# A gated layer's order of pieces on the matmul engine, written anew

## The chip, the cores and the metric

The kernel runs on one NeuronCore of a Trainium2 chip. The core has a matmul engine (PE, with its weight loads shown apart as PEld), a vector engine (DVE), an activation engine (ACT), a general engine (POOL), and queues that issue DMAs (SP, and POOL for gathers and scatters). The engines run side by side; each executes its own instructions in the order in which they were written, and semaphores make one wait for another. Matmul results land in PSUM, which DVE and ACT read; everything else lives in SBUF. The metric is the time of one launch in microseconds (us), the median over launches; a profiled launch is told apart.

## The reference, cut to what matters

The program is a stack of four layers over an activation `x` of 2048 tokens by 256. Each layer normalizes `x` and adds an attention branch and a feed-forward branch. The third layer (`L2`) is the one that is touched. Its attention branch is a gated attention with 64 slots per head, 16 heads:

```python
z = cumlogsumexp(s); g = exp(concat(z[:1], z[:-1]) - z); p = exp(s - z)   # s = clip(x @ Ws, -32, 32)
hk = hk * g_t + k_t * p_t;  ok_t = q_t @ hk          # slot scores, one step per token
pv = softmax(ok)
hv = hv * g_t + p_t * v_t;  ov_t = pv_t @ hv
o  = rmsnorm(ov) * g_norm_weight * silu(x @ Wg)      # then o @ Wo is added to x
```

Its feed-forward branch is itself a small block: a latent attention (16 heads of 16, causal, with rotary parts), a residual, a root-mean-square norm, a shared expert and two of seven routed experts:

```python
h   = x + attention(rmsnorm(x, ln1))
out = h + shared(rmsnorm(h, ln2)) + routed(rmsnorm(h, ln2))
```

## The kernel before, in words

The gated attention is cut into 32 units: 8 pairs of heads times 4 blocks of 512 tokens. The recurrences are written as chunks of 128 tokens, so a unit is a chain of matmuls with small DVE and ACT steps between. Three generators emit it, and each `yield` ends a piece of PE work:

- `gated_supply` (lines 1361 to 1395, pieces "s"): the projections `Wk`, `Ws`, `Wq` of a coming unit (line 1371), the clamp (1381), exponential (1382), running sum `rz` (1383) and its four reciprocals on DVE (1384), and the transposes `kt` and `eT` (`turned`, 1402).
- `gated_unit` (pieces "m"): key scores `sc` (line 1440), values `Wv` (1455), chunk sums `ke` and `ev` (1422), slot scores inside the chunk and between chunks (1475 and 1481, giving `pok`), the product `ok` on DVE (1485), its transposes `okt` (1489), the softmax on DVE and ACT (1493 to 1499), gates `Wg` (1455, silu on ACT 1503), the transposes `pvt` (1507) and `q2` (1511), second scores (1440), and the output `pov` in two steps (1518 and 1525). What follows `pov` is squares on ACT (1535), products and sums on DVE (1536, 1539), and a scale by POOL (1541 to 1548) that finishes the unit's `o`.
- `gated_drain` (pieces "d"): the transposes `ot` of that `o` (line 1561, copied by ACT at 1562) and two halves of `o @ Wo` (1568) added to `x` on DVE (1573).

A list, `GATED` (and `LAST` for the last unit), says in which order the pieces of three chains follow on PE: the unit itself ("m"), the supply of the next unit, the drain of the unit before. Each entry holds the chain, the array size that its matmuls use (A for 128 by 128, B for 64 rows, C for 64 columns), and an assumed length in us. All PE instructions keep the order in which they are emitted; the other engines' orders are chosen by the framework's scheduler from its own estimates.

Other work runs beside the units: `latent_chain` (line 1678) during the first 24, then the routed experts `routed2`, then parts of the next layer. The class `Beside` (line 107) decides before each gated piece whether pieces of that other work go in. It keeps a credit (filled in proportion to the gated time emitted) and a weight per piece. Wide pieces are of kind A; the latent key scores come as narrow pieces E (32 rows, `qk` at 1778 for the maxima, `kq` at 1810 for the exponentials), F (32 columns, `pv` at 1826) and K (the keys, 1737 to 1754). A narrow piece goes in where the array size turns anyway, and at least 1.8 us, by the planner's own lengths (`PIECE`), after the last narrow one. A wide piece has no such distance: among them are the transposes `mxt` (1795), which need the maxima, and the transposes of the latent `pvs` (1836).

At the end of a block of tokens the latent chain emits, as wide pieces: transposes `att` (1853), the projection `op` (1860) added to `xn` on DVE (1865), then the norm (squares on ACT 1690, a sum on POOL 1876 and a power on POOL 490 and 491, the scaling on DVE 1693), the transposes `tr` of the normed rows (552), the router's `lg` (1883, 1889) and the shared expert (1906, 1189).

PSUM is held in pools of four banks: one pool, tag `ps`, for all gated pieces, one, tag `w`, for the latent chain. A piece can start when the bank that was handed out four requests earlier has been read. In SBUF most gated tiles have a single buffer.

Of the kernel before, what the change touches and what calls it, by code (L numbers as in the profile page):

```python
# [7 lines left out]
F32 = mybir.dt.float32  # L8
# [36 lines left out]
class Ring:  # L45
# [40 lines left out]
    ("m", "B", 1.1), ("m", "A", 1.8), ("m", "A", 1.8), ("s", "A", 1.8), ("m", "C", 0.5), ("m", "C", 0.8),  # L86
    ("m", "C", 0.9), ("m", "A", 0.7), ("s", "A", 1.8), ("d", "A", 0.9), ("m", "A", 0.5), ("m", "A", 1.8),
    ("m", "A", 1.8), ("m", "A", 0.5), ("s", "A", 1.8), ("m", "B", 1.1), ("m", "B", 0.8), ("s", "A", 0.5),
    ("m", "A", 1.8), ("d", "A", 1.8), ("s", "A", 0.5), ("d", "A", 1.8),
)  # L90
LAST = (
    ("m", "B", 1.1), ("m", "A", 1.8), ("m", "A", 1.8), ("m", "C", 0.5), ("m", "C", 0.8), ("m", "C", 0.9),
    ("m", "A", 0.7), ("d", "A", 0.9), ("m", "A", 0.5), ("m", "A", 1.8), ("d", "A", 1.8), ("d", "A", 1.8),
    ("m", "A", 1.8), ("m", "A", 0.5), ("m", "B", 1.1), ("m", "B", 0.8), ("m", "A", 1.8),
)
PIECE = {"A": 1.0, "E": 1.3, "F": 2.0, "K": 4.1}
# [10 lines left out]
class Beside:  # L107
# [3 lines left out]
    def __init__(self, pieces, apart=1.8, early=4.0):  # L111
        self.pieces, self.apart, self.early = pieces, apart, early
        self.ahead = next(pieces, None)
        self.now, self.narrow, self.credit, self.before = 0.0, -9.0, 0.0, "A"

    def go(self):
        self.ahead = next(self.pieces, None)

    def between(self, after):

        while self.ahead:
            kind, weight = self.ahead
            turn = self.before != after
            if self.credit < weight - (self.early if turn and kind != "A" else 0.0):
                break
            late = self.credit >= 4.5 + weight and "A" in (self.before, after)
            if kind == "A":
                if "A" not in (self.before, after):
                    break
            elif self.now - self.narrow < self.apart or not (turn or late):  # L130
                break
            self.credit -= weight
            self.order = self.before
            self.go()
            self.now += PIECE[kind]
            if kind != "A":
                self.narrow = self.now
            self.before = {"A": "A", "K": "B" if self.order == "A" else "A"}.get(kind, kind)
# [6 lines left out]
    def finish(self):  # L145
        while self.ahead:
            self.order = self.before
            kind = self.ahead[0]
            self.go()
            self.before = {"A": "A", "K": "B" if self.order == "A" else "A"}.get(kind, kind)  # L150


class Net:
# [1042 lines left out]
    def layer2(self):  # L1196
# [9 lines left out]
        with ExitStack() as ctx:  # L1206
# [8 lines left out]
            def supplied(u):  # L1215
# [5 lines left out]
                units[u] = {"b": b, "w": weights[pair]}  # L1221
                return self.gated_supply(units[u])
# [9 lines left out]
            def run(u, beside, count):  # L1232


                supply = supplied(u + 1) if u + 1 < UNITS else iter(())
                drain = self.gated_drain(units[u - 1]) if u else iter(())
                chains = {"m": self.gated_unit(units[u]), "s": supply, "d": drain}
                order = [p for p in (GATED if u + 1 < UNITS else LAST) if u or p[0] != "d"]
                rate = count / sum(us for _, _, us in order)
                for what, kind, us in order:  # L1240
                    beside.between(kind)
# [5 lines left out]
            for it in (norms[0], supplied(0)):  # L1247
                for _ in it:
                    pass
            with ExitStack() as lctx:  # L1250
# [111 lines left out]
    def gated_supply(self, t):  # L1362
# [15 lines left out]
        nc.scalar.copy(t["kT"], project("Wk"))  # L1378
        yield
# [4 lines left out]
        inverse = lambda c: nc.vector.reciprocal(rz[:, c * P : (c + 1) * P], rz[:, c * P : (c + 1) * P])  # L1384
# [862 lines left out]
```

## Time and profile before

| | us |
|---|---|
| median of 3 launches (2227.93 to 2236.01) | 2228.69 |
| the profiled launch | 2251.34 |
| its span, first to last instruction | 2249.6 |
| PE busy in the span | 1903.3 |
| DVE busy | 1221.3 |
| ACT busy | 894.5 |
| POOL busy | 639.1 |
| the 1000 us from 540 to 1540: PE busy | 941.21 |
| the same: DVE, ACT, POOL busy | 579.45, 443.71, 166.85 |

The page's 40 slices show the gated layer as the stretch from about 490 to 1870 us: PE is busy eight or nine tenths in every slice there, DVE five or six, ACT four, DMA nearly none until 1540. A busy figure of PE counts a matmul from its issue to its modelled end, at whatever clock was granted, so it contains time in which the array ran slowly. A line of the view by waits reads: who waited, for whom, total us, number of times, longest. In the timeline each row is a run of equal instructions with its start, its length, and in brackets the idle time before it and what ended that.

### The profile page before, as it was taken

To read this page: it belongs to the slowest core of one execution; us is meant where nothing else is said; L and a number is where in the kernel's file an instruction comes from. 1 tells how busy PE (TensorE), PEld (TensorE's weight loads), DVE (VectorE), ACT (ScalarE), POOL (GpSimd) and SP (SyncE) were. 2 spreads that over 40 slices of the span, in tenths; PEclk is the share of its full clock that TensorE was granted. 3 is DMA by queue.
4 is the path that set the end of the run, shared out by engine and by line. 5 is a ranking of instruction groups with operands and counts; after the bars stand their busy time and mean duration, and the time that the engine had idled before them with its cause. 6 is when DMAs were issued, how large, how long until landed. Compare 5 with 4: busy or idle time off the path is not lost.

```text
span 2249.6 us, 35179 instructions
## 1 busy us (share of the span) xinstructions
PE 1903.3 (85%) x12844; PEld 1422.2 (63%) x12844; DVE 1221.3 (54%) x3593; ACT 894.5 (40%) x1828; POOL 639.1 (28%) x762
## 2 busy tenths in 40 slices
PE   6843388848999999999999999988889978799995
PEld 2511377726666676667666666666777866578994
DVE  6752367667655665555655566548546574422222
ACT  1340155523434534434444444453345433234321
POOL 5347544451121211112112112111434441022231
PEclk9965699979999999999999999999999989789998
DMA  9944389850000000000000000001433310167696
GB/s 286 306 138 162 130 272 309 282 183 1 8 10 6 8 10 6 6 13 5 6 13 6 3 15 24 6 10 51 135 120 118 109 50 1 41 227 263 216 330 230
DMA packets 145083, 231.46 MB, mean 103 GB/s; under 512 B 15156, under 2 KB 107670, under 8 KB 144758
## 3 DMA queue, kind: packets, MB, share of 16 engines
q1 hardware_dynamic: 130822, 188.74, 26.3%
q0 software_dynamic: 14064, 40.23, 5.2%
q8 instruction: 107, 1.75, 0.3%
q14 instruction: 90, 0.74, 0.1%
HBM read 178.07 MB, written 66.19 MB: 109 GB/s over the span
## 4 chain that ended last, share of the span: by engine, by line
PE 61%; DVE 10%; DMA 7%; POOL 6%; issue 6%; SPq 5%; ACT 4%; POOLq 0%; DVEq 0%; another core or an unknown queue 0%; ACTq 0%
PE pt L1455 7%; PE pj L1371 6%; SPq L469 5%; PE g L1998 5%; PE o L1568 4%; PE kq L1810 3%; PE sc L1440 3%; POOL l_rows L338 3%; PE pov L1525 3%; PE qk L1778 2%; PE gu L1165 2%; PE o L2011 2%; DMA l_rows<-xn,at 2%; DMA r<-l_rows,in_slot 2%; PE pv L1826 2%
## 5 line engine op out<-in xcount | busy, mean ns | idle before, releaser
L446 POOL DMA_INDIRECT l_outs<-y,to x156 | 153.5, 984 | 276.2 <-ACT y L445 157.4
L1785 DVE CUSTOM_DVE_ANT_0 junk<-qk,hide 128x512 f32<-128x512 f32 (+3 forms) x256 | 124.5, 486 | 73.0 <-PE qk L1778 53.3
L1455 PE MATMUL pt<-Wg,xnT 128*128 128x256 f32 x512 | 131.4, 410 | 9.0 <-DVE eF L1381 9.0
L1818 POOL TENSOR_SCALAR_AFFINE_SELECT pr<-pr 128x512 f32<-128x512 f32 x64 | 40.2, 640 | 343.6 <-ACT pr L1815 328.4
L1998 PEld LDWEIGHTS g<-rT,we 128*128 128x128 f32 x1120 | 131.9, 194 | 5.3 <-ACT rT L439 3.2
L1998 PE MATMUL g<-rT,we 128*128 128x128 f32 x1120 | 132.8, 277 | 1.7 <-ACT rT L439 1.7
L396 POOL DMA_INDIRECT r<-l_rows,in_slot x73 | 71.2, 976 | 211.1 <-PE rt L437 99.7
L1455 PE MATMUL pt<-Wv,xnT 128*128 128x256 f32 x512 | 122.8, 390 | 0.0
L408 DVE TENSOR_TENSOR mine<-r,number 128x2 f32<-128x2 f32 (+2 forms) x90 | 16.4, 183 | 195.8 <-DMA r<-l_rows,in_slot 190.6
L1568 PE MATMUL o<-Wo,oT 128*128 128x256 f32 x512 | 122.5, 383 | 0.0
L439 ACT COPY rT<-rt 128x256 f32<-128x256 f32 x156 | 57.9, 372 | 157.9 <-remote 75.8
L1455 PEld LDWEIGHTS pt<-Wg,xnT 128*128 128x128 f32 x512 | 102.3, 207 | 25.5 <-DVE eF L1381 10.0
L1165 PE MATMUL gu<-rT,we 128*128 128x128 f32 x664 | 94.8, 288 | 25.4 <-ACT rT L439 13.4
L1446 DVE TENSOR_TENSOR s<-sc,keep 128x512 f32<-128x512 f32 x128 | 82.7, 683 | 60.2 <-PE sc L1440 59.5
L1384 DVE RECIPROCAL rz<-rz 128x128 f32<-128x128 f32 x128 | 114.6, 926 | 0.3
L1165 PEld LDWEIGHTS gu<-rT,we 128*128 128x128 f32 x664 | 88.8, 200 | 39.5 <-ACT rT L439 21.2
L1455 PEld LDWEIGHTS pt<-Wv,xnT 128*128 128x128 f32 x512 | 95.7, 193 | 16.6 <-PE kq L1810 1.5
L445 ACT ACTIVATE y<-o,share 128x256 f32<-128x256 f32 x156 | 73.6, 472 | 80.6 <-PE o L2011 43.4
L1568 PEld LDWEIGHTS o<-Wo,oT 128*128 128x128 f32 x512 | 97.1, 198 | 10.1 <-issue 1.7
L1815 ACT ACTIVATE pr<-kq 128x512 f32<-128x512 f32 (+1 forms) x192 | 85.7, 531 | 44.4 <-PE kq L1810 44.1
L1458 ACT COPY v<-pt 128x512 f32<-128x512 f32 x64 | 37.6, 588 | 150.5 <-PE pt L1455 150.5
L1810 PE MATMUL kq<-q,kT 32*128 32x128 f32 (+3 forms) x512 | 86.1, 475 | 5.2 <-DVE mx L1785 5.0
(502 smaller groups left out, 4478.3 us busy)
## 6 DMA issues: line engine op xcount, KB each, us to landing
we<-l_packed SPq DMA_DIRECT2D x121, 384.0 KB
we<-l_w SPq DMA_DIRECT2D x70, 512.0 KB
we<-l_wo SPq DMA_DIRECT2D x35, 512.0 KB
l_rows<-none SPq DMA_DIRECT2D x1, 13917.5 KB
r<-l_rows SPq DMA_DIRECT2D x16, 732.5 KB
xn<-l_outs SPq DMA_DIRECT2D x32, 256.0 KB
l_rows<-xn SPq DMA_DIRECT2D x8, 544.0 KB
l_packed<-l_w_gate SPq DMA_DIRECT2D x1, 4096.0 KB
```

Source lines behind the costliest of these rows:

```text
L446: self.no_order(moe["name"] + " back", nc.gpsimd.indirect_dma_start(out=moe["outs"][:, :], out_offset=bass.IndirectOffsetOnAxis(ap=to, axi ...
L469: self.nc.sync.dma_start(out, in_)
L1165: nc.tensor.matmul(ps[:, q, :], we[:, q, k * P : (k + 1) * P], rT[:, k, :], start=(k == 0), stop=(k == KD - 1))
L1371: nc.tensor.matmul(ps, w[n][:, k, :], self.xnT[:, k, t["b"] * T : (t["b"] + 1) * T], start=(k == 0), stop=(k == KD - 1))
L1384: inverse = lambda c: nc.vector.reciprocal(rz[:, c * P : (c + 1) * P], rz[:, c * P : (c + 1) * P])
L1446: nc.vector.tensor_tensor(s, ps[hh], keep4, ALU.mult)
L1455: nc.tensor.matmul(ps[:, i, :], self.xnT[:, k, s : s + P], w[n][:, k, :], start=(k == 0), stop=(k == KD - 1))
L1568: nc.tensor.matmul(ps[:, p, :], of_parity(oT[:, h, c * D : (c + 1) * D], p), wo[:, h, :], start=(h == 0), stop=(h == 1),)
L1785: nc.vector.tensor_tensor_reduce(out=junk[:, :m], in0=tiles[j][:, off : off + m], in1=self.hide[:, T - m :], op0=ALU.add, op1=ALU.max, sca ...
L1810: nc.tensor.matmul(tiles[j][:, BLOCK[i] - off : BLOCK[i] - off + T - i * P], kT[r, i * P : (i + 1) * P], qT[r, i * P :], start=True, stop= ...
L1815: nc.scalar.activation(pr[:, j, off : off + m], tiles[j][:, :m], AF.Exp, scale=0.25)
L1998: nc.tensor.matmul(pt[:, m, :], we[:, q, k * T + m * P : k * T + (m + 1) * P], rT[:, k, :], start=(k == 0), stop=(k == KD - 1),)
```

## The change

The order of pieces in `GATED` and `LAST` is written anew, and so are the order within two of the chains and the rule by which other work goes in.

1. In the unit ("m"), the first half of `Wv` becomes the first piece, ahead of the key scores. It is emitted at the end of the unit before (entry "n"; for the first unit, ahead of the loop). The two halves of `Wg`, two pieces with a yield between, become one piece of 3.6 us.
2. In the supply, the order `Wk`, `Ws`, `Wq`, `kt`, `eT` becomes `Ws`, `Wq`, `eT`, `Wk`, `kt`; the four reciprocals follow one piece each, from the second on.
3. In the list, `ot` moves up to stand behind the second half of `Wv`, the first half of `o @ Wo` goes between the inter-chunk scores and `okt`, the second half between `Wg` and `pvt`; `Ws` moves ahead of the inter-chunk scores; `Wq`, `eT` stand between `pvt` and the second scores, `Wk` between the two steps of `pov`.
4. Each entry gets a fourth field. Where it is 1, a wide piece of other work may go in ahead of the entry on a credit of its weight less 2; elsewhere a wide piece now needs its weight plus 1 (before: its weight everywhere). Narrow pieces may go in as early as before, at a credit of their weight less 4.
5. Distances are kept by kind (`APART`): 1.8 for E, 2.5 for F, 1.5 for K, and for two wide kinds that are now told apart, 3.0 for `mxt` ("X") and 1.5 for the transposes of `pvs` ("Y"). The assumed lengths of E and F change a little.

The matmuls are the same in number and shape, 18764 PE instructions in the program before and after.

```diff
 GATED = (
-    ("m", "B", 1.1), ("m", "A", 1.8), ("m", "A", 1.8), ("s", "A", 1.8), ("m", "C", 0.5), ("m", "C", 0.8),
-    ("m", "C", 0.9), ("m", "A", 0.7), ("s", "A", 1.8), ("d", "A", 0.9), ("m", "A", 0.5), ("m", "A", 1.8),
-    ("m", "A", 1.8), ("m", "A", 0.5), ("s", "A", 1.8), ("m", "B", 1.1), ("m", "B", 0.8), ("s", "A", 0.5),
-    ("m", "A", 1.8), ("d", "A", 1.8), ("s", "A", 0.5), ("d", "A", 1.8),
+    ("m", "B", 1.1, 0), ("m", "A", 1.8, 0), ("d", "A", 0.9, 0), ("m", "C", 0.4, 0), ("m", "C", 0.7, 0), ("m", "C", 1.0, 0),
+    ("s", "A", 1.8, 0), ("m", "A", 0.7, 1), ("d", "A", 1.8, 0), ("m", "A", 0.5, 1), ("m", "A", 3.6, 0), ("d", "A", 1.8, 0),
+    ("m", "A", 0.5, 1), ("s", "A", 1.8, 0), ("s", "A", 0.5, 0), ("m", "B", 1.1, 1), ("m", "B", 0.8, 0),
+    ("s", "A", 1.8, 0), ("m", "A", 1.8, 1), ("n", "A", 1.8, 0), ("s", "A", 0.5, 0),
 )
...
-PIECE = {"A": 1.0, "E": 1.3, "F": 2.0, "K": 4.1}
+PIECE = {"A": 1.0, "X": 0.5, "Y": 0.5, "E": 1.2, "F": 2.2, "K": 4.1}
+APART = {"A": 0.0, "X": 3.0, "Y": 1.5, "E": 1.8, "F": 2.5, "K": 1.5}
...
-    def between(self, after):
+    def between(self, after, wish):
 
         while self.ahead:
             kind, weight = self.ahead
-            turn = self.before != after
-            if self.credit < weight - (self.early if turn and kind != "A" else 0.0):
+            turn, wide = self.before != after, "A" in (self.before, after)
+            if self.now - self.narrow < APART[kind]:
                 break
-            late = self.credit >= 4.5 + weight and "A" in (self.before, after)
-            if kind == "A":
-                if "A" not in (self.before, after):
+            if kind in "AXY":
+                if not wide or self.credit < weight + (-2.0 if wish else 1.0):
                     break
-            elif self.now - self.narrow < self.apart or not (turn or late):
+            elif not turn and not (wide and self.credit >= 4.5 + weight) or self.credit < weight - 4.0:
                 break
             self.credit -= weight
...
-        nc.scalar.copy(t["kT"], project("Wk"))
-        yield
         eF, rz = t["eF"], t["rz"]
         nc.vector.tensor_scalar(eF, project("Ws"), 32.0, -32.0, ALU.min, ALU.max)
         nc.scalar.activation(eF, eF, AF.Exp)
         nc.vector.tensor_tensor_scan(rz, self.one_col.to_broadcast([P, T]), eF, 0.0, ALU.mult, ALU.add)
         inverse = lambda c: nc.vector.reciprocal(rz[:, c * P : (c + 1) * P], rz[:, c * P : (c + 1) * P])
+        yield
+        nc.scalar.mul(t["qT"], project("Wq"), 0.125)
         inverse(0)
         yield
-        nc.scalar.mul(t["qT"], project("Wq"), 0.125)
+        t["eT"] = self.turned(eF, "eT")
         inverse(1)
         yield
+        nc.scalar.copy(t["kT"], project("Wk"))
+        inverse(2)
+        yield
         t["kt"] = self.turned(t["kT"], "kt")
-        inverse(2)
-        yield
-        t["eT"] = self.turned(eF, "eT")
         inverse(3)
...
+        v = wk.tile([P, 4, D], F32, tag="v", name="v")
+        by_tokens("Wv", v, 0, nc.scalar.copy)
+        yield
         s = scores(kT, qT)
         yield
-        v = wk.tile([P, 4, D], F32, tag="v", name="v")
-        for c in (0, 2):
-            by_tokens("Wv", v, c, nc.scalar.copy)
-            yield
+        by_tokens("Wv", v, 2, nc.scalar.copy)
+        yield
...
         for c in (0, 2):
             by_tokens("Wg", g, c, lambda out, ps: nc.scalar.activation(out, ps, AF.Silu))
-            yield
+        yield
...
-                steps.append((self.latent_maxima(*maxima[2:]), list("EEEA")))
+                steps.append((self.latent_maxima(*maxima[2:]), list("EEEX")))
...
-                steps.append((self.latent_values(*values), list("EEEFA")))
+                steps.append((self.latent_values(*values), list("EEEFY")))
```

## The prediction

> **What bounds the kernel now.** First the page: busy time and the slices.
>
> ```profile
> PE 1903.3 (85%) x12844; PEld 1422.2 (63%) x12844; DVE 1221.3 (54%) x3593; ACT 894.5 (40%) x1828; POOL 639.1 (28%) x762
> PE   6843388848999999999999999988889978799995
> PEclk9965699979999999999999999999999989789998
> ```
>
> The gated layer is slices 9 to 33. PE is nearly full there, no other engine is above six tenths: PE's order is the path, and a reordering can only win or lose idle time, slow clock, and turns of the array size. The waits of PE between 540 and 1540 us, where the latent chain runs beside the units, name the idle part (who waited, for whom: us, times, longest):
>
> ```profile
> PE pvt L1507 <- ACT pv L1496: 12.5, 8, 2.2
> PE mxt L1795 <- DVE rz L1384: 12.2, 4, 3.0
> PE pt L1455 <- DVE eF L1381: 9.0, 4, 2.3
> PE mxt L1795 <- ACT pr L1815: 8.0, 9, 2.3
> PE kq L1810 <- DVE mx L1785: 5.0, 12, 0.6
> PE pvt L1836 <- ACT pvs L1832: 3.0, 2, 2.3
> ...
> PE mxt L1795 <- DVE mt L1792: 1.8, 1, 1.8
> ```
>
> All rows of that answer sum to 58. The slow clock is the second part. Stretches before, in and after one wait (length, busy us and count of each engine, granted clock, DMA):
>
> ```profile
> 1037.00:1039.75 2.75, 0.49 (x6) 0.26 (x4) 1.55 (x4) 0.90 (x4) 1.08 (x2) 1.00 0.00 0
> 1039.80:1043.20 3.40, 3.40 (x8) 2.78 (x9) 3.40 (x6) 2.80 (x5) 1.71 (x2) 0.50 0.00 0
> 1043.20:1046.60 3.40, 2.50 (x14) 1.89 (x14) 3.40 (x5) 3.10 (x4) 0.08 (x1) 1.00 0.00 0
> ```
>
> PE stood for 2.26 us, and the next 3.4 us ran at half clock: 1.7 us more. Laying stretches of 3.41 us over the layer, each of the 20 that held 2 us or more of idle time was followed by a half-clock one; of the 29 with 0.9 to 2 us, six were. From 540 to 1540 the mean clock is 0.97, so 30 us are lost that way.
>
> A third part shows in no wait. A group of value scores `kq` follows a group of maxima `qk` and takes over its four PSUM banks one by one as DVE reads them; the gaps stay under what counts as idle. A large group (2048 columns) should take 0.9 us and takes 2.4 to 4.2 when it stands 2 us of PE work behind its `qk`; summed over the layer's groups, against the duration of those that stand 5 us or more behind, the excess is 45 us.
>
> **The change part by part.** Distances below are PE work between two instructions in the built orders, priced by the trace (0.43 us per 512 columns on the full array and pass, a half or a quarter of it for B, C and E, F).
>
> *Turns.* 362 in the layer before, 384 after. Start to start, a turn adds 0.094 us: +2.
>
> *Waits that go.* `mxt` stood 0.1 us behind the last `kq`; now 3.8 to 5.6 lie between. Its 22.0 us (12.2 + 8.0 + 1.8) go. `Wg` no longer waits for a bank that the clamp holds: 9.0. `pvs` gets 1.7 us or more instead of once 0.1: 3.0. Between `okt` and `pvt` lay 3.5 us or more, now 5.2 (`Wg` and half of `o @ Wo`); the chain there (silu, table load, exponential) needed 4.9, so of 12.5 us I leave 4, in the units where DVE still has maxima ahead: 8.5 go. Sum −42.5. Thirteen half-clock stretches followed these: −22.
>
> *What is late next, 1: the feature turn after the latent output.* This decides my forecast. The rows, from the end of `op` on (timelines of PE, DVE and POOL):
>
> ```profile
> 768.18 3.30 PE L1860 MATMUL op<-both,oT 128*128 128x256 f32 x14 [0.24 <-ACT oT L1854]
> ...
> 785.12 1.04 PE L552 MATMUL tr<-ident,xn 128*128 128x128 f32 x8
> ```
> ```profile
> 771.51 0.69 DVE L1865 TENSOR_TENSOR xn<-op,xn 128x512 f32<-128x512 f32 x1 [1.03 <-PE op L1860]
> ...
> 775.89 0.88 DVE L1693 SCALAR_TENSOR_TENSOR xn<-xn,rms,ln 128x256 f32<-128x256 f32 x2 [3.02 <-POOL rms L491]
> ```
> ```profile
> 772.29 2.19 POOL L1876 TENSOR_TENSOR x<-x,xn 128x1024 f32<-128x1024 f32 x1 [12.18 <-DVE xn L1865]
> 774.56 0.19 POOL L490 TENSOR_SCALAR rms<-ms 128x4 f32<-128x4 f32 x1
> 774.84 1.02 POOL L491 TENSOR_TENSOR rms<-rms,neghalf 128x4 f32<-128x4 f32 x1
> ```
>
> The first two normed rows are ready at 776.77, 5.3 us after `op` ends (771.48); before, `tr` came 13.6 us after it. With the new credit rule wide pieces go in several at a time ahead of a flagged entry, and in the built order `tr` stands behind `op` with only half of `o @ Wo` (1.75) between, in three of four blocks, and with nothing in the fourth. Wait 5.3 − 1.75 = 3.5, and 0.3 for the second pair of rows; `lg` now follows `tr` at once and waits 0.5 for the copies; `op` itself waits some 1.6 longer, since on ACT the copy of `att` now stands behind both silus and their table loads (1.28 each). 5.9 × 3, and 8 in the fourth, where reciprocals (0.93 each) also precede the add on DVE: +26. Each block gets about two half-clock stretches, seven in all: +12.
>
> *Late next, 2: `ot`.* The chain from `pov` to a finished `o`:
>
> ```profile
> 1098.92 1.29 DVE L1536 TENSOR_TENSOR o<-pov,g 128x512 f32<-128x512 f32 x2 [2.84 <-ACT sq L1535]
> 1100.12 1.27 DVE L1539 TENSOR_REDUCE ms<-sq 128x4 f32<-128x512 f32 x2
> 1101.47 0.20 POOL L1541 TENSOR_TENSOR rs<-ms,sm 128x8 f32<-128x8 f32 x1 [3.76 <-DVE ms L1539]
> 1101.75 1.64 POOL L1545 TENSOR_TENSOR rs<-rs,neghalf 128x8 f32<-128x8 f32 x1
> 1103.47 2.04 POOL L1548 TENSOR_TENSOR o<-o,rs 128x512 f32<-128x512 f32 x2
> ```
>
> `pov` ended at 1098.4, `o` is done 7.1 later, so the first transpose must start 6.9 behind. Before, 17 to 25 us lay there; now 5.0 to 10.3. The shortfalls of the first 23 units (0.1 to 1.9) sum to 10: +10, too short to slow the clock.
>
> *Late next, 3: exponentials of the keys.* In five units a `kq` falls behind `Wg`, and the built order of ACT puts its four exponentials behind silu, load, softmax exponential, load, silu, load. Walked through with 1.28 per load and 0.6 per activation they end some 3 us after `pv` wants them: +15, and three half-clock stretches, +5. Where a `kq` stands just ahead of `ot`, the copies of `ot` come late for `pok`'s bank, 0.9 in six units: +5.
>
> *Nothing.* `kq` behind `qk`: of the 30 large groups, 15 stand under 2.4 us behind before and 14 after, which gives 45 us both ways. `eT`, `kt`, `Wk` moved: 3.5 us or more to each reader against copies of 0.6; if DVE or ACT were 3 us behind, `kt` would wait. The weight loads on SP follow in a new order (`Ws` before `Wk`), units ahead of use; DMA is at 0.03 there. On POOL only the unit's three scale steps move, behind nothing new.
>
> *Routed experts, 1540 to 1800.* `o` waits for `h` 21 us (17.4 + 1.9 + 1.8). Nine times the new order leaves 0.2 us between a block's `gu` and its `o` (before at least 1.3): silu 0.28, product 0.23 and two hand-overs want about 0.95, and five of these stand behind `Ws`, where a 1.28 load and the 1.22 scan come first: 7 + 11. `ot` adds 6, half-clock 3 more. Some 18 of the old 21 go: +9, between 0 and +18. *The end, to 1870*: a 6.5 us wait of the slot scores for `ke` goes, as ACT now copies both halves ahead of the next layer's operands; those then hold up the exponential: −4, between −10 and +4.
>
> *Sum:* −42.5 − 22 + 2 + 26 + 12 + 10 + 15 + 5 + 5 + 9 − 4 = +15.5, on the profiled launch's 2251.3 (span 2249.6): 2266.8. The median of the launches shown is 22.6 lower: **2244 us**.
>
> [...] The change has 12 more loads. [...]
>
> **The rivals.** *Paid from the hidden stall (faster).* The waits at `ot`, `pvt` and `op` fall between a `qk` and its `kq` and give DVE time to free the banks. Place: the 30 large `kq` groups; price: a group at 2 us loses 2.6, one at 3.2 loses 0.6. If all reach 3.2, 33 us of the 45 come back: 2244 − 33 = 2211. It decides once they gain half a us each on average (15 us). For it: the stalls are real and many units have such a pair. Against: the big new waits, at `tr`, have no `qk` open around them.
>
> *Moved one for one (no change).* DVE's reciprocals (0.93, four a unit) bound both orders; what `mxt` and `Wg` lose, `pvt` and `okt` get, so that the waits and clock that go (64.5) and the latent terms that come (26 + 12 + 10 + 15 + 5 + 5 + 2 = 75) cancel; only the routed part and the end are left, 2251.3 + 9 − 4 − 22.6 = 2234. For it: DVE precedes each of the waits that go. Against: PE has 2 to 5 us more distance at each.
>
> *The routed part breaks down (much slower).* Several rounds at a time empty the four-deep gather: each of some 38 blocks waits 1 us more: 2244 + 38 = 2282.
>
> **How the numbers follow.** A measurement here cannot tell less than about 0.5%, 11 us. Forecast 0.46, paid from stalls 0.32, one for one 0.17, breakdown 0.05. The forecast's own range is 2230 to 2265 (the latent terms ±20%, routed and end by their bounds). To leave no more than 2 in 10 out: 2202 to 2272. Faster 0.32; same 0.17; slower 0.51.
>
> **What would show it.** Right: `mxt` and `Wg <- eF` gone from the waits; `tr <- DVE xn` four times at 3 to 7 us with half clock behind it; `ot <- POOL o` in a dozen units, under 2 us; `pv` waiting for exponentials or their POOL mask. Wrong: `tr` without a wait, or the busy time of `kq` (86.1 before) fallen by 20 or more.

## The result, and the profile after

The changed kernel takes 2246.36 us (median of 12 launches, 2238.88 to 2251.93) against 2231.31 us for the kernel before (12 launches beside it): the ratio is 1.0066, with a 95% interval of 1.0050 to 1.0083, so 15 us more. The forecast was 2244.

Its profiled launch took 2246.59 us (span 2244.9), which is *less* than the 2251.34 us of the profiled launch before. That comparison misleads. In the trace of before, the first projection of the gated layer starts at 483.4 us, in the trace of after at 459.1: the layers ahead, which the change does not touch, happened to take 24 us longer. From the first projection of the layer to the end of the launch, the one took 1766.2 us and the other 1785.8, 19.6 more; the medians say 15, and single launches spread by some 13 us. The stages in the table below are therefore counted from that first projection. First the page of the changed kernel, busy time and slices:

```profile
PE 1914.4 (85%) x12844; PEld 1426.5 (64%) x12844; DVE 1220.4 (54%) x3585; ACT 913.8 (41%) x1848; POOL 637.6 (28%) x762
PE   6843499669999899998999899987889888799995
PEclk9965699879999899999999899998999989789997
```

The matmuls are the same (x12844 in both pages), yet PE is busy 11 us longer. As busy time runs from issue to a modelled end, this says that matmuls ran slowly (clock) or stood inside a group, not that there is more work. ACT has 19 us more, of which 15 are twelve more table loads (142 against 130) of 1.28.

The waits of PE from 540 to 1540 us, beside the latent chain (who waited, for whom: us, times, longest). As the layer starts 24 us earlier in this trace, the last rows of such a view reach into the routed part:

```profile
PE tr L549 <- DVE xn L1696: 15.4, 4, 5.5
PE kq L1813 <- DVE mx L1788: 9.7, 17, 1.5
PE op L1863 <- ACT oT L1857: 8.1, 3, 2.7
PE ot L1564 <- POOL o L1551: 3.5, 7, 0.9
...
PE mxt L1798 <- ACT pr L1818: 2.2, 3, 1.1
```

The first four rows of before (`pvt`, `mxt`, `Wg`, `mxt`: 41.7 us) are gone but for 2.2. At the top stands a wait that was not there, `tr`, four times, once for each block of tokens, as forecast.

The next table divides the launch by stage, from the traces. "Idle" is the sum of PE's gaps above 0.15 us; "clock" is half the time that the records show at half clock; "rest" is what is left. Units 0 to 22 are the stretch from the first `pov` of unit 0 to that of unit 23.

| us | before | after |
|---|---|---|
| first projection to first `pov` | 44.3 | 48.4 |
| units 0 to 22 (latent chain beside) | 994.8 | 1004.3 |
| of these: idle / clock / rest | 59.1 / 30.7 / 905.0 | 47.1 / 35.8 / 921.3 |
| units 23 to 28 (mostly routed experts) | 266.0 | 277.3 |
| from the first `pov` of unit 29 to the end of the launch | 461.1 | 455.8 |

So beside the latent chain 12 us of idle time were won, and 5 us of clock and 16 us of "rest" lost. More than half of that rest is no loss, because the borders of the table cut the two orders at different places. In the new order 16 more matmuls of `o @ Wo` and 16 more of the shared expert stand ahead of the first `pov` of unit 23; before, they stand behind it. At their mean lengths in the stage they are an estimated 9 us. With such differences taken off at each border, the stage beside the latent chain is about 1 us longer than before, units 23 to 28 about 16 us longer, the end 3 us shorter and the start 5 us longer.

Of the 7 us of rest that remain, 2 are for the 22 turns more (384 against 362, at 0.094 us each in the trace of before); the others are PE standing inside groups, in gaps that count as busy. The rows of a few groups show where, over the gated layer (busy us, mean ns | idle before), first of before, then of after:

```profile
L1810 PE MATMUL kq<-q,kT 32*128 32x128 f32 (+3 forms) x512 | 86.1, 475 | 5.2 <-DVE mx L1785 5.0 <-ACT pr L1815 0.2
L1826 PE MATMUL pv<-pr,both 128*32 128x128 f32 (+3 forms) x512 | 37.8, 436 | 0.0
L1561 PE MATMUL ot<-ident,o 128*128 128x128 f32 x248 | 32.5, 274 | 0.0
L1889 PE MATMUL lg<-rw,a2T 128*128 128x7 f32 x64 | 8.2, 263 | 0.0
```

```profile
L1813 PE MATMUL kq<-q,kT 32*128 32x256 f32 (+3 forms) x512 | 88.9, 478 | 9.9 <-DVE mx L1788 9.7
L1829 PE MATMUL pv<-pr,both 128*32 128x128 f32 (+3 forms) x512 | 37.8, 436 | 0.0
L1564 PE MATMUL ot<-ident,o 128*128 128x128 f32 x248 | 36.4, 282 | 6.6 <-POOL o L1551 5.9 <-DVE s L1446 0.7
L1892 PE MATMUL lg<-rw,a2T 128*128 128x7 f32 x64 | 12.8, 337 | 0.0
```

`kq` is busy 2.8 us longer and waits 9.7 us for the maxima instead of 5.0. `ot` took 3.9 us more with the same work; in units 0 to 22, with half clock taken off, it is 2.6. `lg` took 4.6 us more, but that is half clock, which the table has under "clock". `pv` took exactly as long and never waited.

One block's output in the changed kernel, from the timelines of PE, ACT, DVE and POOL (start, length, row, and the idle time before with its releaser):

```profile
750.63 5.47 PE L1863 MATMUL op<-both,oT 128*128 128x256 f32 x16 [2.66 <-ACT oT L1857]
755.94 1.89 PE L1571 MATMUL o<-Wo,oT 128*128 128x256 f32 x8
761.14 2.06 PE L549 MATMUL tr<-ident,xn 128*128 128x128 f32 x8 [3.31 <-DVE xn L1696]
763.13 0.62 PE L1886 MATMUL lg<-rb,ones 1*128 1x28 f32 x2
763.68 3.58 PE L1892 MATMUL lg<-rw,a2T 128*128 128x7 f32 x16
```

```profile
748.21 1.28 ACT L1506 ACT_TABLE_LOAD   x1
749.51 0.60 ACT L1506 ACTIVATE g<-pt 128x512 f32<-128x512 f32 x1
750.00 1.07 ACT L1857 COPY oT<-att 128x512 f32<-128x512 f32 x2
```

```profile
756.14 0.69 DVE L1868 TENSOR_TENSOR xn<-op,xn 128x512 f32<-128x512 f32 x1 [1.41 <-PE op L1863]
...
760.51 1.67 DVE L1696 SCALAR_TENSOR_TENSOR xn<-xn,rms,ln 128x256 f32<-128x256 f32 x4 [1.95 <-POOL rms L488]
```

```profile
756.91 2.18 POOL L1879 TENSOR_TENSOR x<-x,xn 128x1024 f32<-128x1024 f32 x1 [20.06 <-DVE xn L1868]
759.17 0.19 POOL L487 TENSOR_SCALAR rms<-ms 128x4 f32<-128x4 f32 x1
759.45 1.02 POOL L488 TENSOR_TENSOR rms<-rms,neghalf 128x4 f32<-128x4 f32 x1
```

`op` waits 2.66 us, because the copies of the transposed `att` (done at 747.97) stand on ACT behind a table load and a silu of the gates. Behind `op` there is only 1.75 us of other PE work, while the way from `op` over DVE, POOL and DVE to the normed rows takes 5.0 us. PE stands 3.3 us at `tr`, and `lg` then takes 3.58 us instead of 2.05. The stretches of the clock around it (length; busy time of PE, PEld, DVE, ACT, POOL; granted clock; DMA):

```profile
757.80:761.20 3.40, 0.09 (x2) 0.09 (x1) 1.38 (x3) 2.21 (x10) 3.06 (x5) 1.00 0.00 0
761.45:764.86 3.41, 3.41 (x15) 2.94 (x15) 0.73 (x2) 2.35 (x5) 0.80 (x1) 0.50 0.00 0
764.86:768.28 3.42, 3.42 (x17) 3.42 (x17) 0.03 (x1) 0.68 (x2) 0.00 (x0) 0.50 0.00 0
768.28:771.69 3.41, 3.41 (x6) 1.24 (x6) 2.80 (x20) 0.03 (x1) 0.14 (x1) 0.50 0.00 0
```

Three stretches at half clock follow the one wait: 5.1 us lost behind 3.3 us of standing.

### The profile page after: what moved, and what is told of

The parts are those of the page before. It is cut to its first block, busy times and chain, and to the rows that moved or that the text cites. A ratio compares the mean times of both kernels' runs of the same rounds, so it can differ in the third digit from the quotient of the medians.

```text
span 2244.9 us, 35193 instructions
## 1 busy us (share of the span) xinstructions
PE 1914.4 (85%) x12844; PEld 1426.5 (64%) x12844; DVE 1220.4 (54%) x3585; ACT 913.8 (41%) x1848; POOL 637.6 (28%) x762
## 3 DMA queue, kind: packets, MB, share of 16 engines
q8 instruction: 107, 1.75, 0.3%
## 4 chain that ended last, share of the span: by engine, by line
PE 59%; DVE 10%; DMA 8%; POOL 8%; issue 6%; SPq 5%; ACT 5%; POOLq 0%; DVEq 0%; another core or an unknown queue 0%; ACTq 0%
PE pt L1455 8%; PE pj L1373 7%; SPq L466 5%; PE o L1571 4%; PE g L2001 4%; PE kq L1813 3%; POOL l_rows L335 3%; PE pov L1528 2%; PE sc L1440 2%; PE qk L1781 2%; DMA r<-l_rows,in_slot 2%; DVE junk L1788 2%; PE o L2014 2%; PE pv L1829 2%; PE gu L1162 1%
## 5 line engine op out<-in xcount | busy, mean ns | idle before, releaser
L1571 PE MATMUL o<-Wo,oT 128*128 128x256 f32 x512 | 130.8, 401 | 0.0
L1455 PE MATMUL pt<-Wv,xnT 128*128 128x256 f32 x512 | 128.8, 396 | 0.0
L434 PE MATMUL rt<-ident,r 128*128 128x128 f32 x312 | 65.2, 292 | 64.1 <-DMA r<-l_rows 58.6
L1455 PE MATMUL pt<-Wg,xnT 128*128 128x256 f32 x512 | 119.3, 387 | 0.0
L549 PE MATMUL tr<-ident,xn 128*128 128x128 f32 x160 | 36.0, 370 | 90.7 <-DVE xn L516 47.9
L1571 PEld LDWEIGHTS o<-Wo,oT 128*128 128x128 f32 x512 | 102.2, 208 | 16.4 <-issue 3.3
L1455 PEld LDWEIGHTS pt<-Wg,xnT 128*128 128x128 f32 x512 | 97.2, 195 | 12.9 <-issue 0.3
L1818 ACT ACTIVATE pr<-kq 128x512 f32<-128x512 f32 (+1 forms) x192 | 86.2, 531 | 43.4 <-PE kq L1813 43.0
L1162 PEld LDWEIGHTS gu<-rT,we 128*128 128x128 f32 x664 | 88.5, 197 | 20.5 <-ACT rT L436 10.6
```

The costliest lines, as they stand in the source:

```text
L1162: nc.tensor.matmul(ps[:, q, :], we[:, q, k * P : (k + 1) * P], rT[:, k, :], start=(k == 0), stop=(k == KD - 1))
L1455: nc.tensor.matmul(ps[:, i, :], self.xnT[:, k, s : s + P], w[n][:, k, :], start=(k == 0), stop=(k == KD - 1))
L1571: nc.tensor.matmul(ps[:, p, :], of_parity(oT[:, h, c * D : (c + 1) * D], p), wo[:, h, :], start=(h == 0), stop=(h == 1),)
L1818: nc.scalar.activation(pr[:, j, off : off + m], tiles[j][:, :m], AF.Exp, scale=0.25)
```

## The experiments

The theory is that of the prediction: each wait of PE is the difference between the time that DVE, ACT and POOL need from a producer to a consumer and the PE work that the order puts between the two; the new rule removes it at `mxt` and the flags (the fourth field) create it at `tr`. The main rivals are "moved one for one" (the other engines are late by their own work, so a wait that goes comes back at the next piece) and "paid from the hidden stall". The runs were made in three sets, each beside runs of the kernel before on the same chip; in the second set the time of before was 2248 us, not 2231. In the four traces of that set the gated layer starts at 479 to 483 us, in those of the first at 460 to 462, so the difference lies in the part ahead of the layer. So the ratio to before within the set is what counts, and it is given in us of 2231.

| run | ratio to before (95%) | us against before |
|---|---|---|
| the changed kernel | 1.0066 (1.0050 to 1.0083) | +15 |
| `tr` alone kept apart | 0.9992 (0.9982 to 1.0002) | −2 |
| no flag anywhere | 0.9855 (0.9840 to 0.9871) | −32 |
| no flag beside the latent chain | 0.9925 (0.9905 to 0.9945) | −17 |
| no flag beside the routed experts | 0.9996 (0.9986 to 1.0007) | −1 |
| new list, old rule | 1.0000 (0.9983 to 1.0017) | 0 |
| old list, new rule without flag | 0.9844 (0.9827 to 0.9861) | −35 |
| before, with a distance for `mxt` alone | 0.9850 (0.9813 to 0.9888) | −33 |
| old list, new rule, narrow pieces 3.2 apart | 0.9959 (0.9942 to 0.9975) | −9 |
| the same at 2.6, with `tr` apart | 1.0018 (1.0004 to 1.0032) | +4 |
| old list, new rule, routed pieces at their weight | 0.9833 (0.9801 to 0.9865) | −37 |
| old list, new rule, `pvt` later | 0.9748 (0.9714 to 0.9783) | −56 |
| the last two together | 0.9742 (0.9708 to 0.9777) | −58 |

### The flags: `tr` alone, and all wide pieces one at a time

The first run gives the piece with `tr` a kind of its own, which must stand 6 us behind the last wide piece:

```diff
+APART: "T": 6.0, counted from the last wide piece
-                yield from tagged(self.experts2(values[0]))
+                after = self.experts2(values[0])
+                yield "A", 1.0
+                next(after)
+                yield "T", 1.0
+                next(after)
+                yield from tagged(after)
```

> Theory (the prediction's): the transposes tr of the latent output stand too close behind op, and that decides. Here tr alone is held 6 us behind the last wide piece; built distances op to tr become 7.8, 7.8, 7.8 and 8.1 us of PE work (changed kernel: 1.7 three times and 0), all else nearly as in the changed kernel. The changed kernel's profile has 15.4 us of waits of tr and 18.8 us lost to half clock in the stretches right behind them (three of 10.24 us and one of 6.83 us at half rate, the end of the last three-window one not counted whole); so 2246 - 34 = 2212, between 2202 and 2222: faster than the kernel before. Rival (moved one for one): PE only waits for DVE and ACT somewhere else, the waits come back at the next piece, 2238 to 2248.

Measured: 2231.48 us against 2232.55 for before, so 17 us below the changed kernel by the ratios, half of what was expected and between the two ranges. The waits of this run, 540 to 1540 us, show where the other half went:

```profile
PE op L1870 <- ACT oT L1864: 8.1, 3, 2.7
PE sc L1442 <- DVE q L1516: 7.2, 3, 2.4
...
PE o L1188 <- DVE u L1920: 4.6, 4, 1.4
```

`tr` no longer waits (15.4 us gone), but the rest of the batch, `lg`, `gu` and the shared expert's output, still follows in one go behind it. The second scores `sc` now wait 7.2 us for DVE, and the shared expert's `o` 4.6 instead of 0.9. In units 0 to 22 the idle time falls by 4.4 us only, and the clock loss by 10. Neither theory is right alone: the wait at `tr` is one of distance, but new waits of 7.2 and 4.6 us stand at `sc` and in the rest of the batch.

The second run takes the flag away everywhere, one number:

```diff
-                if not wide or self.credit < weight + (-2.0 if wish else 1.0):
+                if not wide or self.credit < weight + 1.0:
```

> The flag of the entries is without effect here: every wide piece needs its weight plus 1, so wide pieces go in one at a time, beside the units and in the routed part as well. Built distances op to tr 6.1, 6.1, 4.4, 8.1. Theory: as in the run with tr kept apart, -34, a little less for the 4.4 (1 us and a half-clock stretch, +3), and the routed part loses its pairs of gu and o 0.2 us apart and their waits: of the +11 us that the profile shows for the units 23 to 28 against before, half to all, -5 to -11. 2246 - 31 - 8 = 2207, between 2197 and 2217. Rival (moved): 2238 to 2248. Rival (batches are good for the routed part, where they keep the gather ahead): the routed units become longer than in the changed kernel, 2220 or more.

Measured: 2202.06 us, within the theory's range (2197 to 2217), 47 us below the changed kernel on one scale. So the rest of the change, without its flags, makes the kernel 32 us faster than before. Units 0 to 22 take 967.8 us instead of 1004.3, with 28.8 us of idle time instead of 47.1, and the wait of `tr` is 0.7. (Of the 36 us between the two, an estimated 5 are work of the shared expert that stands behind the border again.) The `op` wait stays at 8.1, since it comes from ACT's order.

Two more runs say where the flags cost, by a switch for the planner of one stage:

```diff
-                if not wide or self.credit < weight + (-2.0 if wish else 1.0):
+                if not wide or self.credit < weight + (-2.0 if wish and self.flags else 1.0):
...
-                latent = self.latent = Beside(self.latent_chain())
+                latent = self.latent = Beside(self.latent_chain(), False)   # first run
-            routed = Beside(routed)
+            routed = Beside(routed, False)                                  # second run
```

> Changed kernel with the flag without effect beside the latent chain alone (units 0 to 23); in the routed part and the end it acts. The run with the flag off everywhere took 2202 against 2246; its profile against that of the changed kernel: units 0 to 22 36 us shorter, the start 5, units 23 to 28 10, the rest of the launch 8 longer. Theory: nearly all of the 44 lies beside the latent chain: 2246 - 41 = 2205, between 2199 and 2213. Rival (batches cost as much in the routed part): 2220 to 2232.

> Changed kernel with the flag without effect beside the routed experts alone (units 24 to 29). Theory: 10 us come back in the routed units (waits of o for h), of which the end gives some 8 away, as in the run with the flag off everywhere: 2246 - 2 to - 10, so 2236 to 2245. Rival (batches cost as much in the routed part): 2220 to 2230.

Measured: 0.9925 and 0.9996, or 31 and 16 us below the changed kernel; together 47, as much as without any flag. The effects add, and the expectation put too little on the routed part: 41 was expected beside the latent chain, 2 to 10 in the routed part. On the scale of 2231 the two runs stand at 2215 and 2230: the first just above the range of its theory, the second in the range of its rival (batches cost as much in the routed part). The stage of units 23 to 28 by windows, first in the changed kernel, then without the flag in this stage:

```profile
1511.70:1789.10 277.40, 239.13 (x1638) 194.52 (x1638) 155.79 (x541) 122.94 (x240) 98.03 (x101) 0.95 0.32 102
```

```profile
1530.50:1787.10 256.60, 225.76 (x1626) 186.36 (x1626) 152.61 (x540) 121.91 (x238) 97.63 (x100) 0.99 0.35 110
```

The stage is 21 us shorter, 13 of it in busy time; the clock is 0.99 instead of 0.95, which is 10 us of the 21. The waits of the experts' `o` for `h` barely differ (19.6 and 18.6 us); what went is idle time elsewhere and the clock, and which step of the batches causes that stays open.

### The list and the rule, each alone

The new list, chains and pieces with the class `Beside` of the kernel before, and the other way round:

```diff
 new list, old rule:  GATED, LAST and the generators of the changed kernel; Beside, PIECE and kinds of the kernel before
 old list, new rule:  GATED, LAST and the generators of the kernel before; Beside, PIECE, APART and kinds of the changed kernel,
+                    beside.between(kind, 0)
```

> The changed kernel's list, chains and pieces, with the rule of the kernel before for other work (one wide piece at each credit of 1, 1.8 us between narrow ones, mxt at once behind kq). Built: kq to mxt 0.1 in 13 of 15, op to tr 6.1 to 8.1. Theory: the wait of tr goes (-34 and, with single wide pieces, -5 in the routed part), the wait of mxt comes back, smaller than before as the four reciprocals no longer stand together: 8 to 22 us and 4 to 10 of clock. 2246 - 39 + 22 = 2229, between 2217 and 2241. Rival (the list itself is what costs, by ot and the hidden stall of kq): 2240 to 2260.

> The kernel before with its own list and its own order inside the chains, and only the new rule by which other work goes in, with no flag set (wide pieces at weight plus 1; distances 3.0 for mxt, 1.5 for pvs, 2.5 for F). Built: mxt stands 3.1 to 4.5 us behind kq (0.1 before), op to tr 5.6 to 8.7, everything else as before. Theory: the 22.0 us of mxt waits and 3.0 of pvs go, with the half clock behind them (six stretches of 3.4 us, 10 us); what the list removes (Wg 9.0, pvt 12.5) stays: 2231 - 22 - 3 - 10 = 2196, between 2188 and 2208. Rival (one for one): DVE's reciprocals hold PE up at the next piece that needs DVE, and it stays at 2225 to 2235.

Measured: 2231.28 and 2197.37 us, both within the theory's ranges (2229 and 2196 were expected). With the run without flags this makes a square: the list is worth nothing by the old rule (0), and nothing or a little loss by the new one (−32 against −35); the rule without flags is worth 35 with the old list and 32 with the new; the flags cost 47. Under the old rule, with the new list, `mxt` waits 29.9 + 1.8 us, more than the 22.0 of before and more than the 8 to 22 that the expectation had put there; its total came right although this term was wrong.

That the distance of `mxt` is what the rule gains was tried in the kernel before alone:

```diff
-                steps.append((self.latent_maxima(*maxima[2:]), list("EEEA")))
+                steps.append((self.latent_maxima(*maxima[2:]), list("EEEX")))
...
-                if "A" not in (self.before, after):
+                if "A" not in (self.before, after) or kind == "X" and self.now - self.narrow < 3.0:
```

> The kernel before with one distance more: mxt at least 3.0 us behind the last narrow piece (built 3.1 to 4.5 us behind kq instead of 0.1; op to tr 5.4 to 7.2; nothing else of the new rule). Theory (this distance is what the old list with the new rule gained, 35 us): 22 us of waits and about 10 of half clock go: 26 to 36 us below the kernel before on the same chip. Rival (the other parts of the rule, a wide piece at weight plus 1 and the distances of F and pvs, did a good part): 10 to 22 us below.

Measured: 0.9850, or 33 us, within the range of the theory (26 to 36); the runs spread more than others (2187.5 to 2215.0), so the interval is wide. The waits from 540 to 1540 us:

```profile
PE pvt L1507 <- ACT pv L1496: 14.4, 12, 1.8
PE kq L1810 <- DVE mx L1785: 5.0, 12, 0.6
...
PE pt L1455 <- DVE eF L1381: 4.5, 2, 2.3
```

No `mxt` is left, and `pvt` and `kq` wait about as before (12.5 and 5.0). In units 0 to 22 the idle time falls from 59.1 to 36.4 us, by all that `mxt` had waited, and the clock loss from 30.7 to 23.9: the wait was not handed on. "Moved one for one" falls here.

### The hidden stall

The prediction counted 45 us that the `kq` groups stand inside themselves, and its second case would have paid the change from there. The next two runs take the old list with the new rule and widen the distance between narrow pieces:

```diff
-APART = {"A": 0.0, "X": 3.0, "Y": 1.5, "E": 1.8, "F": 2.5, "K": 1.5}
+APART = {"A": 0.0, "X": 3.0, "Y": 1.5, "E": 3.2, "F": 2.5, "K": 1.5}   # second run: "E": 2.6, and "T": 6.0 as above
```

> The old list with the new rule and no flag (2197 us), and 3.2 us instead of 1.8 between narrow pieces of kind E. Built: all 30 large kq groups stand 3.3 us or more behind their qk (15 of them 1.7 to 2.4 before), turns 392 instead of 366, op to tr 1.7 in the first and last block (5.6 or more without). Theory (the hidden stall is a wait for the banks that the maxima still hold): of the 45 us counted in kq, 33 or more go; turns +2, two waits of tr with their half clock +15: 2197 - 33 + 17 = 2181, between 2172 and 2191. Rival (what I count as stall is how long such small matmuls take, or DVE holds PE up elsewhere): 2197 + 17 and a little less, 2205 to 2215.

> The old list with the new rule and no flag, 2.6 us between pieces of kind E, and tr of the latent output at least 6 us behind the last wide piece. Built: 28 of the 30 large kq groups 2.9 us or more behind qk, the two others 2.8; op to tr 7.8 to 9.5; turns 391. Theory: 2197 - 30 + 2 = 2169, between 2161 and 2181, the fastest of all. Rival (the stall does not depend on the spacing): 2197 to 2205.

Measured: 0.9959 and 1.0018, 26 and 39 us *slower* than the old list with the new rule at 1.8. On the scale of 2231 they stand at 2222 and 2235, above the ranges of theory and rival alike. The theory fails, in an instructive way. The row of `kq`, first at 1.8, then at 3.2:

```profile
L1807 PE MATMUL kq<-q,kT 32*128 32x128 f32 (+3 forms) x512 | 84.9, 475 | 5.5 <-DVE mx L1782 5.0 <-ACT pr L1812 0.4
```

```profile
L1807 PE MATMUL kq<-q,kT 32*128 32x128 f32 (+3 forms) x512 | 63.6, 476 | 1.4 <-DVE mx L1782 1.0
```

The stall was real, and 21 us of it went. But these are the longest waits, 540 to 1540 us, first at 1.8, then at 3.2:

```profile
PE pvt L1504 <- ACT pv L1493: 16.3, 13, 1.8
PE kq L1807 <- DVE mx L1782: 5.0, 12, 0.6
PE sc L1437 <- DVE q L1508: 3.5, 4, 1.7
```

```profile
PE pvt L1504 <- ACT pv L1493: 16.1, 15, 1.5
PE turn L1399 <- DVE s L1443: 9.8, 4, 3.0
PE sc L1437 <- DVE q L1508: 7.8, 5, 2.9
PE tr L549 <- DVE xn L1690: 6.6, 2, 3.3
PE pok L1478 <- ACT ke L1427: 6.4, 4, 2.0
```

In units 0 to 22 the idle time rises from 36.3 to 69.0 us, the clock loss from 15.4 to 25.6, and the rest falls from 904.7 to 888.2. Only the 6.6 of `tr` (and some clock) had been allowed for. The time that PE stood inside `kq` has gone, and more than as much has come at `turn`, `sc` and `pok`, each of which wants a result or a bank from DVE or ACT; the clock loss grows too. That the one causes the other is argued, not shown: the wider distance also moves the narrow pieces to other places and adds turns (392 instead of 366). Why DVE is later at those places was not tried.

### A version that beats both

Two edits on the old list with the new rule. The routed pieces go in at their weight again:

```diff
-                if not wide or self.credit < weight + (-2.0 if wish else 1.0):
+                if not wide or self.credit < weight + self.more:
...
-            routed = Beside(routed)
+            routed = Beside(routed, 0.0)   # self.more; 1.0 beside the latent chain
```

> The old list with the new rule and no flag, except that routed pieces go in at their weight, as before, and not at weight plus 1. In the run of the old list with the new rule the units 23 to 28 took 277.8 us against 266.0 before. Theory (those 12 us are the later entry of the routed pieces): 35 + 10 = 45 us below the kernel before, 40 to 50. Rival (they only move between the routed units and the end): 32 to 38 below.

Measured: 0.9833 (0.9801 to 0.9865), 37 us below before; 35 without the edit. That is the rival's range, and the stage agrees, since the routed units gain 4 us, not 12; the interval of the total alone (30 to 44 us) would not exclude the low end of the theory.

The other edit moves two pieces of the list:

```diff
-    ("m", "A", 1.8), ("m", "A", 0.5), ("s", "A", 1.8), ("m", "B", 1.1), ("m", "B", 0.8), ("s", "A", 0.5),
-    ("m", "A", 1.8), ("d", "A", 1.8), ("s", "A", 0.5), ("d", "A", 1.8),
+    ("m", "A", 1.8), ("s", "A", 1.8), ("m", "A", 0.5), ("d", "A", 1.8), ("m", "B", 1.1), ("m", "B", 0.8),
+    ("s", "A", 0.5), ("m", "A", 1.8), ("s", "A", 0.5), ("d", "A", 1.8),
```

> The old list with the new rule and no flag, and two pieces moved: the projection Wq of the supply stands ahead of pvt (5.3 us of PE work from okt to pvt instead of 3.5, as in the changed kernel's list), and the first half of o @ Wo goes between pvt and the second scores. Theory (distance is what each wait wants): of the 16.3 us that pvt waits for the exponential 13 go, and sc does not take them over, as it keeps 1.8 us: 35 + 13 = 48 us below the kernel before, 42 to 54. Rival (one for one: ACT and DVE are late by their own queues and PE stands at the next piece): 30 to 38 below.

> Both edits of the two runs above together. Theory (they lie in different places and add): 55 to 60 us below the kernel before. Rival: the better one of the two alone.

Measured: 2170.94 us, 0.9748 (0.9714 to 0.9783) for the second edit alone, 56 us below before (48 to 64 by the interval; 42 to 54 was expected); 0.9742 for both, which cannot be told from it. The waits of the second edit's run, 540 to 1540 us, have no `pvt` any more, and `sc` has not taken it over:

```profile
PE kq L1807 <- DVE mx L1782: 7.8, 16, 0.9
PE o L1337 <- DVE h L1332: 5.6, 3, 3.5
```

The `o` row belongs to the routed part, which this trace reaches before 1540. Units 0 to 22 take 942.6 us (idle 21.9, clock 11.9), against 994.8 before and 1004.3 after the change. Two pieces were moved at once here, so what each is worth is not known.

## Why the prediction was right, and where it was not

The sum was +15.5 us and the measured change +15. The direction and the mechanism held: the new rule takes the waits at `mxt` away, and the flags bring new ones at the feature turn. That the size came out is luck to a large part. By the table the stages seem to fit: +10.5 forecast beside the latent chain (measured +9.5), +9 in the routed part (+11.3), −4 at the end (−5.3), nothing at the start (+4.1). With equal work between the borders they are about +1, +16, −3 and +5. So the forecast was some 10 us too high beside the latent chain and 12 too low in the routed part and at the start, and the errors cancel.

- *Waits that go, −42.5.* Right: `mxt` 22.0 to 2.2, `Wg` 9.0 to 0, `pvs` 3.0 to 0, `pvt` 12.5 to 0, so −44.3. (All rows of before sum to 58.8, not 58.) The run with the `mxt` distance alone shows that most of the gain lies there.
- *The feature turn after the latent output, +26.* The step was right in place and mechanism, down to the row: 1.75 us of work between, 3.3 us of wait (3.5 forecast), `op` delayed by ACT's order (8.1 us in three blocks, where 1.6 each had been added to 0.2 each), `lg` delayed behind `tr`. It measured 15.4 at `tr` and some 7 more at `op`, 22 to 23 in all, and 18.8 of clock. The run without flags beside the latent chain gets 31 us back; the waits of `op` are the same there.
- *The clock, −22 + 12 + 5 beside the latent chain.* Mis-sized: −5 forecast, +5 measured (30.7 to 35.8). Of the 18 half-clock stretches in units 0 to 22 before, 12 followed waits that went (13 were counted). Behind `tr` came eleven instead of seven: three in three blocks and two in the fourth, 18.8 us in all. Two follow the waits of `op`, and one or two more than before those of `kq`; neither was costed.
- *`ot`, +10.* Too high by half: in units 0 to 22 it is 2.3 us of waits for `o` and 2.6 inside the transposes. Over the whole layer the waits are 5.9 us, and the sum had a further 6 for `ot` in the routed part.
- *The exponentials of the keys, +15 and +5 of clock.* Wrong. `pv` was busy 37.8 us in both, without a wait. In five groups the last exponential ends within 0.4 us of `pv`'s start: just in time, not 3 us late. The step that walked ACT's built order with durations from before came out too late. What the loads did delay is `op`, which had been costed less.
- *`kq`, nothing.* Wrong: its waits rose by 4.7 us and its busy time by 2.8. (The 45 us counted as hidden contain the 5.0 of waits that the rows name.) The spacing behind `qk` alone does not set the stall: two groups that start 2.5 us behind their `qk` took 4.6 and 4.8 us after, longer than two of the three slowest before (4.4, 4.4 and 5.3), which start 1.7 us behind. This miss takes back part of the last one.
- *`pok` behind the copies of `ot`, +5.* 0.6 measured.
- *The routed part, +9.* Too low, and wrong in its parts: of the old 21 us of waits for `h`, 18 were to go and 18 to come; 19.6 are there, and the loss is elsewhere in idle time (37.3 against 30.3 in the stage) and clock (13.7 against 8.5). The 16 us more at equal work are what the flags cost there by their own run.
- *The start.* Its +4.1 was not costed; `okt` waits 2.3 us there for DVE's product. In the two runs without flags beside the latent chain the start takes 43.3 and 43.4 us, not 48.4, so it comes with the flags too.

Of the rivals, "paid from the hidden stall" did not happen, and in the run at 3.2 us it was not to be had that way: 21 us went from `kq`, and 33 us of idle time came elsewhere. "Moved one for one" thus fits that stall, and not `mxt` and `pvt`, whose waits vanish when distance is put in. The clock terms of the prediction rest on its count of stretches, and the other traces agree with it: in the 14 profiles, from 480 to 1880 us, every one of the 170 stretches of 3.41 us with 2 us or more of idle time was followed by one at half clock (20 of 20 before, 16 of 16 after); in the trace of before only 3 stretches were idle throughout, and 33 ran at half clock. For the table loads the prediction took 1.28 us each, and the ACT rows of the changed kernel above show the same: the silu starts 0.02 us after its load of 1.28 ends, and that load starts 0.01 us after the exponential ahead of it ends (748.20).

## What to carry to other kernels

When an order is set by hand, write down for each pair of producer and consumer how long the other engines need (here 5 us from `op` to `tr`, 3 from `kq` to `mxt`, 5 from `okt` to `pvt`) and how much work lies between; one distance that is too short can cost nearly all that a whole rule is worth (here 33 of 35 us), and a rule that lets pieces in together can cost more. A change with several parts should be taken apart in a square of runs before it is kept or dropped: here one part was worth 35 us and another cost 47. A stall that hides inside busy time is no store of gain as such: before spending it, ask what the engine that causes it will be late for next. And before a stage of one trace is compared with the same stage of another, count whether both hold the same work.

## What the runs showed of the hardware

In these traces the clock also dropped where the records show PE busy all the time. In the kernel before, the 16 matmuls of `lg` at 788.18 us have seven columns and start 0.12 us apart; two of 28 columns stand ahead of them. Two stretches around them:

| stretch, us | PE busy | `lg` in it | granted clock |
|---|---|---|---|
| 787.20 to 790.60 | 3.40 | 2.24 | 1.00 |
| 790.60 to 794.00 | 3.40 | 0 | 0.50 |

PE has no idle time in the first, and the next runs at half clock. In the 14 profiles, from 480 to 1880 us, 24 stretches at full clock hold 2.0 us or more of `lg` (here and in the next layer, seven or eight columns; counted from each matmul's start to the next one's) and less than 0.2 us of idle time. Of these, 19 were followed by half clock, among them all 18 with 2.09 us or more; of the 64 with 1 to 2 us, none was. So half clock followed 18 of 18 of these stretches with 2.09 us or more of `lg`, as it followed 170 of 170 with 2 us or more of idle time; how the clock is set was not shown.

This fits the length of the half clock at `tr`. After the three waits of 3.3 us in the changed kernel, where `lg` follows `tr` at once, it lasted 10.24 us, three stretches, although PE was busy in the second and third; three such waits in the run without flags beside the routed experts did the same. In the run at 3.2 us, where `turn` or `pvt` follows `tr`, the half clock behind two such waits lasted 3.41. Where no wait stands ahead of `lg`, in the runs with `tr` apart or without flags, three of four are followed by no half clock. Stretches at half clock were followed by another with less than 2 us of `lg`, or with none; what decides there stays open.

The clock also differed between runs where the order did not. The last two runs have the same 6510 matmuls in the same order in units 0 to 22, and the same idle time, 21.9 us; they lost 11.9 and 20.5 us there to half clock. With 0.9 to 2 us of idle time in a stretch, 6 of 29 were followed by half clock before, 5 of 26 after, 105 of 451 in all 14 profiles; what decides it was not found.
